# PSUM as a ring of four two-bank tiles, and a rearranged head, in a convolution kernel made of lookups

## The chip, the core and the metric

The kernel runs on one core of one Trainium2 chip. Such a core has five engines that run at the same time, each through its own list of instructions and strictly in the order of that list: TensorE (PE in the profile) multiplies matrices, VectorE (DVE) and ScalarE (ACT) work elementwise, GpSimd (POOL) too, and SyncE (SP) issues DMAs. PE has a second row, PEld, for loading the weights that stay in the array during a matmul. PE writes only to PSUM, a small memory of eight banks; here a bank holds 512 numbers of 32 bits on each of 128 partitions. The engines wait for one another by semaphores. The metric is the device time of one execution in microseconds (us).

## The reference

The input x has 16 images of 256 channels and 28x28 pixels. A group norm is followed by two "lookup" convolutions with batch norms, a squeeze-and-excitation gate and two residual sums:

```
def amm_conv3x3(x, centroids, w_sub):          # centroids: 256 channels, k=16, s=9
    p = 3x3 patches of x                       # per channel and pixel: 9 numbers
    d = |p|^2 - 2 p.centroids + |centroids|^2  # distance to each of 16 centroids
    attn = softmax(-d)                         # over the 16
    lut = einsum('cks,cso->cko', centroids, w_sub)
    return einsum('bnck,cko->bno', attn, lut)

out = amm_conv3x3(group_norm(x), centroids1, w_sub1)
out = relu(batch_norm1(out))
out = amm_conv3x3(out, centroids2, w_sub2)
out = batch_norm2(out)
out = out * sigmoid(relu(mean(out) @ w1 + b1) @ w2 + b2)
return x + relu(out + group_norm(x))
```

## The kernel before

**The work is cut into blocks.** A block is one layer, one image, one half of the channels (`hh`) and one half of the image's rows (`t`, 14 rows, 392 pixels, the `N` of the code). There are 2 x 16 x 4 = 128 blocks. The list `blocks` numbers them from 0; I call them block 0, block 1 and so on. The four blocks of one image and layer are needed together, because the sum over the channels is done by a Strassen-like scheme with seven products in place of eight.

**What happens to a block.** `patches` reads the shifted rows of the normalised image, which lies in HBM in `home1` or `home2`, into one of two tiles `pts` in SBUF, six DMAs for each half block. `logits` makes the 16 distances of a quarter of the block's channels: 16 small matmuls, each in a 32x32 corner of the array, into four PSUM banks. `exps` takes the exponential on ACT, bank by bank, and so frees the banks. `num_b` sums the exponentials (the denominators of the softmax, and the ninth tap); `split_b` on ACT and `join_b` on DVE sort the two apart, `recip_dve` inverts, `spread` shuffles the reciprocals to the right partitions. `num_a` makes the other eight taps' numerators, a quarter of the channels at a time, into two banks. They leave PSUM by `copy_a` on ACT (scaled later by `scale_q` on POOL) or by `scale_a` on DVE, scaled on the way. The results are the tiles `q`. `mix` subtracts q tiles of two blocks on POOL, `product` multiplies q tiles by weights (18 matmuls for a full one) into one accumulator bank, and `acc_copy` or `acc_add` takes it out.

**PSUM.** All of these take their banks from one pool, `p_ring`, by `bank(name)` (L103): eight tiles of one bank, handed out in turn. Whoever takes the next tile waits until the tile that was handed out eight turns earlier has been read.

**The order is written out by hand.** `at(cl, sub, f, ...)` (L847) files a job under a step `cl` and a place `sub` within it. At the end all jobs are issued in the order of (step, place), and this is the order in each engine's list. A block takes two steps: in each, `logits` and `exps` for two quarters (places 0.1 to 0.22). Block j starts at step 2j. Its `num_b` comes at step 2j+2, place 1.3, two `num_a` at 1.35, `split_b` 1.4, `copy_a` 1.45, `join_b` 1.5, `recip_dve` 1.6; its other two `num_a` come at step 2j+3, place 1.0, with `scale_a` at 1.1 and the `scale_q` of the first two at 1.8. A `product` stands at place 2.0 of most steps. So an even step has two `logits`, a `num_b`, two `num_a` and a product, an odd step two `logits`, two `num_a` and a product.

**The next image's group norm** is threaded into this: `load_x` (SP), `gn_stats` (DVE), `gn_mean` and `gn_var` (a small matmul each, DVE, and in `gn_var` also POOL: `rsqrt`, L235 and L236, then L317 and L318), `gn_apply` on ACT with what POOL made, and `to_home1` on SP, which writes the normalised image to HBM. The patches of the image's first block read it back.

**The head.** Before the first logits the program loads image 0 in two halves, normalises each (`norm0`), centres the centroids of the two channel halves (`center_wd`: squares on DVE, matmuls with `nhalf_sb` on PE, sums on DVE), fills the `pts` tiles with ones and writes image 0 to `home1`. In before, `center_wd(1)` stands at step 0, place 1.95, the weights `A11` of the first product are loaded at step 1, and image 1 at step 2.

## Time and profile before

| what | value |
|---|---|
| median of three runs | 2734.56 us (2731.55 to 2735.21) |
| the profiled execution | 2732.52 us, its span 2731.0 us |
| PE busy | 2663.6 us, 98% of the span |
| POOL busy | 2075.3 us, 76% |
| DVE busy | 1718.3 us, 63% |
| ACT busy | 1445.9 us, 53% |
| granted PE clock, mean | 0.995 |

The span runs from the first to the last instruction; 1.5 us of the profiled execution lie outside it. A row of the timeline view has the start, the time that the row's instructions covered, the engine, the line of the kernel, the operation, what it writes and reads, how many instructions were merged into the row, and in brackets how long the engine had been idle before them and what ended that. Matmul ends are modelled in the profile, so a busy PE is not necessarily a PE at its peak. `<-issue` means that the profile shows nothing that the engine waited for.

### The profile page before, as it was taken

The page shows a single profiled execution, that of the slowest core. Times are in us where ns is not written, and L with a number is a line of the kernel's source. Part 1 is how long each engine was busy: PE and PEld are TensorE (multiplying, and loading weights), DVE is VectorE, ACT ScalarE, POOL GpSimd, SP SyncE. Part 2 cuts the span into 40 slices and gives each one's busy share as a digit, 9 for nine tenths or more (in the row PEclk, how much of TensorE's full clock was granted, in tenths as well). Part 3 has the DMA queues.
Part 4 walks back from the last instruction along what each step waited for, and adds up shares of the span by engine and source line. Part 5 has one row for each costly group of instructions (what it writes and reads, how often), then busy time and mean ns, then how long its engine had stood idle before and what let it go on. Part 6 is the DMA issues. An engine that isn't in the chain of part 4 may idle for free. (4 is left out here: it accounts for less than half of the span.)

```text
span 2731.0 us, 87796 instructions
## 1 busy us (share of the span) xinstructions
PE 2663.6 (98%) x36984; PEld 1293.3 (47%) x36984; DVE 1718.3 (63%) x3943; ACT 1445.9 (53%) x3233; POOL 2075.3 (76%) x1425
## 2 busy tenths in 40 slices
PE   5899999999999999999999999999999999999998
PEld 2444544444444444444444444444444444444444
DVE  4765655566565556655567766666766676766674
ACT  3445444544445554555545555656556656556653
POOL 4856787766887677876678887788887788887787
PEclk9999999999999999999999999999999999999999
DMA  9665667766566666666585555545555445555441
GB/s 198 150 143 159 144 156 197 190 148 129 151 163 160 172 155 140 172 166 160 127 180 119 106 121 121 115 102 116 115 122 125 111 105 115 115 124 125 110 105 57
DMA packets 223624, 374.50 MB, mean 137 GB/s; under 512 B 30633, under 2 KB 194009, under 8 KB 223225
## 3 DMA queue, kind: packets, MB, share of 16 engines
q1 hardware_dynamic: 216280, 334.87, 53.3%
q0 software_dynamic: 6944, 33.95, 3.7%
q8 instruction: 295, 4.83, 0.8%
q14 instruction: 105, 0.85, 0.1%
HBM read 288.93 MB, written 79.80 MB: 135 GB/s over the span
## 5 line engine op out<-in xcount | busy, mean ns | idle before, releaser
L369 ACT ACTIVATE e<-lg 128x392 f32<-128x392 f32 x1920 | 778.2, 528 | 803.9 <-PE lg L357 797.7
L495 POOL TENSOR_TENSOR qp<-qp,qp 128x784 f32<-128x784 f32 x512 | 938.2, 1861 | 26.0 <-DVE qp L478 26.0
L486 PE MATMUL acc<-qp,w_S 128*128 128x392 f32 x2048 | 704.4, 494 | 0.9 <-POOL qp L495 0.9
L467 POOL TENSOR_TENSOR qp<-qp,rb 128x784 f32<-128x784 f32 x256 | 471.5, 1859 | 181.3 <-DVE rb L459 173.5
L357 PE MATMUL lg<-pt,wd 32*32 32x392 f32 x16384 | 541.2, 504 | 21.1 <-DMA pt<-home 16.2
L459 DVE STREAM_SHUFFLE rb<-r 128x392 f32<-128x392 f32 x1024 | 551.7, 603 | 0.0
L486 PEld LDWEIGHTS acc<-qp,w_S 128*128 128x128 f32 x2048 | 386.7, 190 | 299.1 <-issue 17.4
L486 PE MATMUL acc<-qp,w_A 128*128 128x392 f32 x1536 | 521.2, 492 | 0.0
L438 DVE SCALAR_TENSOR_TENSOR r<-nb,kst,r 128x392 f32<-128x392 f32 x128 | 79.8, 624 | 572.9 <-ACT r L429 557.6
L404 PE MATMUL na<-e,cwa 64*32 64x392 f32 x8192 | 412.1, 495 | 9.0 <-issue 9.0
L486 PEld LDWEIGHTS acc<-qp,w_A 128*128 128x128 f32 x1536 | 291.8, 190 | 213.8
L418 PE MATMUL nb<-e,cwb 64*32 64x392 f32 x8192 | 373.8, 496 | 3.9 <-issue 3.4
L467 POOL TENSOR_TENSOR qo<-qo,rb 128x392 f32<-128x392 f32 x128 | 131.0, 1024 | 301.6 <-DVE rb L455 301.4
L357 PEld LDWEIGHTS lg<-pt,wd 32*32 32x32 f32 x16384 | 232.8, 103 | 257.3 <-issue 170.9
L444 DVE RECIPROCAL r<-r 128x392 f32<-128x392 f32 x128 | 331.9, 2593 | 0.0
L478 DVE TENSOR_TENSOR qp<-na,rb 128x392 f32<-128x392 f32 x512 | 253.3, 554 | 68.4 <-PE na L404 58.9
L404 PEld LDWEIGHTS na<-e,cwa 64*32 64x32 f32 x8192 | 147.0, 106 | 236.4 <-ACT e L369 122.0
L418 PEld LDWEIGHTS nb<-e,cwb 64*32 64x32 f32 x8192 | 144.1, 107 | 226.2 <-issue 140.5
L472 ACT COPY qp<-na 128x392 f32<-128x392 f32 x512 | 211.8, 513 | 9.1 <-PE na L404 9.1
L429 ACT ACTIVATE r<-nb,kst 128x392 f32<-128x392 f32 x128 | 87.6, 684 | 105.6 <-PE nb L418 100.8
L375 ACT COPY e<-lg 128x392 f32<-128x392 f32 x128 | 52.9, 501 | 149.8 <-PE lg L357 149.8
L493 POOL TENSOR_TENSOR qo<-qo,qo 128x392 f32<-128x392 f32 x128 | 130.8, 1022 | 1.7
(149 smaller groups left out, 1747.9 us busy)
## 6 DMA issues: line engine op xcount, KB each, us to landing
pt<-home SPq DMA_DIRECT2D x768, 209.0 KB
pt<-home SPq DMA_DIRECT2D x756, 104.5 KB
home<-xpad SPq DMA_DIRECT2D x31, 899.0 KB
xt<-in_x SPq DMA_DIRECT2D x30, 784.0 KB
out_dram<-y SPq DMA_DIRECT2D x32, 392.0 KB
w_S<-d_wS SPq DMA_DIRECT2D x4, 576.0 KB
st<-in_wsub SPq DMA_DIRECT2D x4, 512.0 KB
st<-d_wa SPq DMA_DIRECT2D x16, 128.0 KB
```

Source lines behind the costliest of these rows:

```text
L357: nc.tensor.matmul(bk[32 * c : 32 * c + 32, :N].rearrange("p (r w) -> p r w", w=W), lhsT=wts["wd", u["hh"]][32 * i : 32 * i + 32, mm, c, : ...
L369: nc.scalar.activation(eg[:, i, :], bk[:, :N], AF.Exp, scale=2.0)
L404: nc.tensor.matmul(bs[r][32 * i : 32 * i + 32, :N], lhsT=wts["cwa", u["hh"]][64 * r : 64 * r + 64, mm, i, :], rhs=es[64 * r : 64 * r + 64, ...
L418: nc.tensor.matmul(bs[r][32 * i : 32 * i + 32, :N], lhsT=wts["cwb", u["hh"]][64 * r : 64 * r + 64, mm, i, :], rhs=es[64 * r : 64 * r + 64, ...
L444: nc.vector.reciprocal(u["r"], u["r"])
L459: nc.vector.stream_shuffle(rb[:, r, :], u["r"], mask_of(2 * mm + r))
L467: nc.gpsimd.tensor_tensor(q, q, u.pop(("rb", mm)), ALU.mult)
L472: nc.scalar.copy(u["q", 2 * mm + r], bk[:, :N])
L478: nc.vector.tensor_mul(u["q", 2 * mm + r], bk[:, :N], rb[:, r, :])
L486: nc.tensor.matmul(accs[key][:, :N], lhsT=wl[w][:, k, :], rhs=us["q", k], start=first and n == 0, stop=last and n == len(ks) - 1,)
L493: nc.gpsimd.tensor_tensor(out_u["q", 8], in0["q", 8], in1["q", 8], ALU.subtract)
L495: nc.gpsimd.tensor_tensor(pair(out_u, mm), pair(in0, mm), pair(in1, mm), ALU.subtract)
```

## The change

The pool `p_ring` has four tiles of two banks in place of eight tiles of one. `logits`, `num_a` and `num_b` put two banks' worth into one tile, and `exps`, `wide_copy`, `copy_a` and `scale_a` read both banks (128x784) with one instruction where two read one bank each (128x392). Everything else that asks for a bank (`product`, the group norm's sums, the centring, the gate) now gets a two-bank tile and uses its first bank. The matmuls stay the same, in the same banks of a group.

In the head, the weights `A11` are loaded at the start and the second half of `cwa` and `cwb` at step 4, the other way round from before. The tile `pts[1]` is filled by ACT, not POOL. The centring of the second half is cut in two, the squares ahead of step 0 and the rest in step 1. Block 0's `num_b` and all that follows from it comes one step earlier (step 1 where it was step 2; its other `num_a` at step 2 where they were at 3). Image 1 is loaded at the end of step 3 (before: step 2), its `gn_stats` and `gn_mean` stand at step 5 (before: 4), its `gn_var` at step 6, place 0.25 (before: step 4, place 2.2), `gn_apply` at step 6, place 0.3 (before: step 5, place 0.3), and both `to_home1` at step 6, place 0.4 (before: step 5, places 0.9 and 1.9).

The diff, without its plainly repeated parts:

```diff
--- before.py
+++ after.py
@@ -94,14 +94,17 @@
     const = ctx.enter_context(tc.tile_pool(name="const", bufs=1))
     dram = ctx.enter_context(tc.tile_pool(name="dram", bufs=1, space=DRAM))
     small = ctx.enter_context(tc.tile_pool(name="small", bufs=2))
-    p_ring = ctx.enter_context(tc.tile_pool(name="p_ring", bufs=8, space=PSUM))
+    p_ring = ctx.enter_context(tc.tile_pool(name="p_ring", bufs=4, space=PSUM))
 
     gmat = const.tile([P, P], F32, name="gmat")
     make_block_diagonal(nc, gmat, 8)
     ctx.enter_context(tc.manual_schedule())
 
+    def banks(name):
+        return p_ring.tile([P, 2, 512], F32, tag="ps", name=name)
+
     def bank(name):
-        return p_ring.tile([P, 512], F32, tag="ps", name=name)
+        return banks(name)[:, 0, :]
 
     def view(t, off, dims):
         return bass.AP(t.tensor, t.offset + off, [list(d) for d in dims])
@@ -193,7 +196,7 @@
     kst = load(konst, "kst")
     load_cw(0, 0)
     load_wd(None, 1)
-    load_cw(0, 1)
+    load_w(0, "A11")
     vecs = load(vec, "vecs", nc.gpsimd)
     w1_sb = const.tile([P, NB, 2 * RED], F32, name="w1_sb")
     w2_sb = const.tile([2 * RED, P], F32, name="w2_sb")
@@ -352,7 +355,9 @@
     def logits(u, mm):
         bs = []
         for i in range(4):
-            bk = bank("lg")
+            if i % 2 == 0:
+                bs.append(banks("lg"))
+            bk = bs[-1][:, i % 2, :]
             for c in range(4):
                 nc.tensor.matmul(
                     bk[32 * c : 32 * c + 32, :N].rearrange("p (r w) -> p r w", w=W),
@@ -360,19 +365,18 @@
                     rhs=u["pt", mm // 2][32 * i : 32 * i + 32, 4 * (mm % 2) + c, :].rearrange("p (r w) -> p r w", w=PW)[:, :, :W],
                     start=True, stop=True,
                 )
-            bs.append(bk)
         u["lg", mm] = bs
 
     def exps(u, mm):
         eg = epool.tile([P, 4, N], F32, tag="e", name="e")
         for i, bk in enumerate(u.pop(("lg", mm))):
-            nc.scalar.activation(eg[:, i, :], bk[:, :N], AF.Exp, scale=2.0)
+            nc.scalar.activation(eg[:, 2 * i : 2 * i + 2, :], bk[:, :, :N], AF.Exp, scale=2.0)
         u["e", mm] = eg
 
...
@@ -397,12 +401,12 @@
         nc.scalar.activation(eg, eg, AF.Exp, scale=2.0)
 
     def num_a(u, mm):
-        bs = [bank("na") for _ in range(2)]
+        bs = banks("na")
         es = u["e", mm]
         for i in range(4):
             for r in range(2):
                 nc.tensor.matmul(
-                    bs[r][32 * i : 32 * i + 32, :N],
+                    bs[32 * i : 32 * i + 32, r, :N],
                     lhsT=wts["cwa", u["hh"]][64 * r : 64 * r + 64, mm, i, :],
                     rhs=es[64 * r : 64 * r + 64, i, :],
                     start=True, stop=True,
@@ -410,13 +414,13 @@
         u["na", mm] = bs
 
     def num_b(u):
-        bs = [bank("nb") for _ in range(2)]
+        bs = banks("nb")
         for mm in range(4):
             es = u["e", mm]
             for i in range(4):
                 for r in range(2):
                     nc.tensor.matmul(
-                        bs[r][32 * i : 32 * i + 32, :N],
+                        bs[32 * i : 32 * i + 32, r, :N],
                         lhsT=wts["cwb", u["hh"]][64 * r : 64 * r + 64, mm, i, :],
                         rhs=es[64 * r : 64 * r + 64, i, :],
                         start=(mm == 0), stop=(mm == 3),
@@ -424,7 +428,7 @@
         u["nb"] = bs
 
     def split_b(u):
-        b0, _ = u["nb"]
+        b0 = u["nb"][:, 0]
         r = rpool.tile([P, N], F32, tag="r", name="r")
         nc.scalar.activation(r, b0[:, :N], AF.Identity, bias=zero, scale=m_hi)
         q = qs["one"][u["qi", 4]]
@@ -433,7 +437,7 @@
         u["q", 8] = q
 
     def join_b(u):
-        _, b1 = u.pop("nb")
+        b1 = u.pop("nb")[:, 1]
         r, q, w = u["r"], u["q", 8], u["w"]
         nc.vector.scalar_tensor_tensor(
             r, b1[:, :N], m_lo, r, op0=ALU.mult, op1=ALU.add, accum_out=wsum[:, w : w + 1]
@@ -467,15 +471,15 @@
         nc.gpsimd.tensor_tensor(q, q, u.pop(("rb", mm)), ALU.mult)
 
     def copy_a(u, mm):
-        for r, bk in enumerate(u.pop(("na", mm))):
+        for r in range(2):
             u["q", 2 * mm + r] = pair(u, mm)[:, r, :]
-            nc.scalar.copy(u["q", 2 * mm + r], bk[:, :N])
+        nc.scalar.copy(pair(u, mm), u.pop(("na", mm))[:, :, :N])
 
     def scale_a(u, mm):
         rb = u.pop(("rb", mm))
-        for r, bk in enumerate(u.pop(("na", mm))):
+        for r in range(2):
             u["q", 2 * mm + r] = pair(u, mm)[:, r, :]
-            nc.vector.tensor_mul(u["q", 2 * mm + r], bk[:, :N], rb[:, r, :])
+        nc.vector.tensor_mul(pair(u, mm), u.pop(("na", mm))[:, :, :N], rb)
 
     accs = {}
 
@@ -884,21 +888,22 @@
                     at(g + 1, 0.9, wide_exp, u, mm)
                 else:
                     at(g + p, 0.12 + 0.1 * q, exps, u, mm)
-        at(g + 2, 1.3, num_b, u)
-        at(g + 2, 1.4, split_b, u)
-        at(g + 2, 1.5, join_b, u)
-        at(g + 2, 1.6, recip_dve, u)
-        at(g + 2, 1.7, spread, u, 4)
-        at(g + 2, 1.71, scale_q, u, 4)
+        h = g + 2 if j else 1
+        at(h, 1.3, num_b, u)
+        at(h, 1.4, split_b, u)
+        at(h, 1.5, join_b, u)
+        at(h, 1.6, recip_dve, u)
+        at(h, 1.7, spread, u, 4)
+        at(h, 1.71, scale_q, u, 4)
         for mm in range(2):
-            at(g + 2, 1.35, num_a, u, mm)
-            at(g + 2, 1.45, copy_a, u, mm)
-            at(g + 3, 1.8 + 0.01 * mm, spread, u, mm)
-            at(g + 3, 1.8 + 0.01 * mm, scale_q, u, mm)
+            at(h, 1.35, num_a, u, mm)
+            at(h, 1.45, copy_a, u, mm)
+            at(h + 1, 1.8 + 0.01 * mm, spread, u, mm)
+            at(h + 1, 1.8 + 0.01 * mm, scale_q, u, mm)
         for mm in range(2, 4):
-            at(*((g + 2, 1.8) if mm == 2 else (g + 3, 0.05)), spread, u, mm)
-            at(g + 3, 1.0, num_a, u, mm)
-            at(g + 3, 1.1, scale_a, u, mm)
+            at(*((h, 1.8) if mm == 2 else (h + 1, 0.05)), spread, u, mm)
+            at(h + 1, 1.0, num_a, u, mm)
+            at(h + 1, 1.1, scale_a, u, mm)
 
     for l in range(2):
         for b in range(B):
@@ -942,14 +947,14 @@
                         for r in range(2):
                             at(g + 12 + o + (o and r), (1.72, 2.9)[r] if o == 0 else (1.805, 2.9)[r], to_home2, b, o, r)
                 if b + 1 < B:
-                    at(*((g - 1, 2.6) if b else (2, 1.65)), load_x, b + 1)
+                    at(*((g - 1, 2.6) if b else (3, 1.66)), load_x, b + 1)
                     for q in range(NB):
-                        at(g + (1 + q if b else 4), 0.3, gn_stats, b + 1, q)
-                    at(g + (3 if b else 4), 2.1, gn_mean, b + 1)
-                    at(g + 4, 2.1 if b else 2.2, gn_var, b + 1)
+                        at(g + (1 + q if b else 5), 0.3, gn_stats, b + 1, q)
+                    at(g + (3 if b else 5), 2.1, gn_mean, b + 1)
+                    at(*((g + 4, 2.1) if b else (6, 0.25)), gn_var, b + 1)
                     for q in range(NB):
-                        at(g + 5, 0.9 if b else 0.3, gn_apply, b + 1, q)
-                        at(g + 5, 1.9 if b or q else 0.9, to_home1, b + 1, q)
+                        at(*((g + 5, 0.9) if b else (6, 0.3)), gn_apply, b + 1, q)
+                        at(*((g + 5, 1.9) if b else (6, 0.4)), to_home1, b + 1, q)
             else:
                 last = b == B - 1
                 at(*((g + 11, 0.6) if last else (g + 13, 2.6)), load_x, b, last)
@@ -970,7 +975,7 @@
                     at(g + 11, 0.65, flags)
                     at(g + 12, 2.9, flag_sum)
 
-    at(1, 1.65, load_w, 0, "A11")
+    at(4, 0.6, load_cw, 0, 1)
     at(3, 1.65, load_w, 0, "S3")
     at(3, 1.65, load_w, 0, "A22")
     at(6, 0.6, load_w, 0, "A12")
@@ -1030,20 +1035,34 @@
         gn_var(0, k, 1)
         gn_apply(0, k)
 
-    def center_wd(hh):
-        center(wts["wd", hh].rearrange("p a b c -> p (a b c)"), 512)
+    def flat_wd(hh):
+        return wts["wd", hh].rearrange("p a b c -> p (a b c)")
+
+    squares = []
+
+    def center_wd1(part):
+        wf = flat_wd(1)
+        if part == 0:
+            squares.extend(center_sq(wf, c0, 256) for c0 in (0, 256))
+        else:
+            for c0 in (0, 256):
+                center_add(wf, c0, 256, squares[c0 // 256])
+            center_mean(wf, 512)
 
     nc.vector.memset(pts[0][:, :4], 1.0)
+    nc.scalar.activation(
+        pts[1], xpads[0][:, :PTW].unsqueeze(1).to_broadcast([P, 8, PTW]), AF.Identity, bias=1.0, scale=1.0
+    )
     norm0(0)
     for i in range(2):
         to_home1(0, 0, i)
     nc.vector.memset(pts[0][:, 4:], 1.0)
-    nc.gpsimd.memset(pts[1], 1.0)
-    center_wd(0)
+    center(flat_wd(0), 512)
     norm0(1)
-    at(0, 1.95, center_wd, 1)
     at(-0.5, 0.7, to_home1, 0, 1)
-    at(0, 1.96, setup_bn)
+    at(-0.4, 0.7, center_wd1, 0)
+    at(1, 1.25, center_wd1, 1)
+    at(1, 1.96, setup_bn)
     for t in hpads:
         at(1, 1.95, nc.gpsimd.memset, t, 0.0)
 ```

## The prediction

> **What bounds the kernel now.** I read the page first: which engine is full, and where along the span.
>
> ```profile
> PE 2663.6 (98%) x36984; PEld 1293.3 (47%) x36984; DVE 1718.3 (63%) x3943; ACT 1445.9 (53%) x3233; POOL 2075.3 (76%) x1425
> ...
> PE   5899999999999999999999999999999999999998
> ```
>
> PE is busy in every slice but the first ones and the last; 67 us of its span are idle. Second, the waits of PE alone, cut at 205 us. Up to there:
>
> ```profile
> PE lg L357 <- DMA pt<-home: 14.5, 4, 8.0
> PE gnp L298 <- DVE gn_mv L293: 9.1, 2, 5.7
> PE na L404 <- issue: 7.8, 4, 4.1
> ...
> PE acc L486 <- POOL w_S L188: 3.7, 1, 3.7
> ```
>
> and after it:
>
> ```profile
> PE lg L357 <- DVE hpad L523: 3.5, 4, 1.3
> PE nb L418 <- issue: 3.4, 2, 1.8
> ```
>
> The second list has 13 us in all. So visible idle time is to be had in the first 200 us only, and what the ring does to the other 2500 us must lie inside the busy time. Third, therefore, the timeline of one ordinary odd step:
>
> ```profile
> 1130.57 2.03 PE L357 MATMUL lg<-pt,wd 32*32 32x392 f32 x64
> 1131.56 3.23 ACT L369 ACTIVATE e<-lg 128x392 f32<-128x392 f32 x8 [5.48 <-PE lg L357]
> 1132.53 0.18 PEld L404 LDWEIGHTS na<-e,cwa 64*32 64x32 f32 x16 [0.64 <-ACT e L369]
> ...
> 1134.10 0.93 PE L486 MATMUL acc<-qo,w_S 128*128 128x392 f32 x2
> ```
>
> The first `num_a` starts 1.96 us after the logits, behind an ACT exponential that frees its banks. But in 52 of 119 even steps after 205 us `num_b` also starts at 1.96, although ACT began 0.06 earlier there (0.93 against 0.99 after the logits). So the usual limit is the logits' own end, 2.03, less 0.07; the exponentials come next, close behind.
>
> Fourth, POOL and ACT around the place to which the next image's `gn_var` moves:
>
> ```profile
> 67.80 0.22 POOL L235 TENSOR_SCALAR rs_t<-gn_var 128x2 f32<-128x2 f32 x1 [2.47 <-DVE nrm L315]
> ...
> 73.65 4.82 POOL L467 TENSOR_TENSOR qp<-qp,rb 128x784 f32<-128x784 f32 x2 [4.22 <-ACT xpad L324]
> 78.41 1.03 POOL L493 TENSOR_TENSOR qo<-qo,qo 128x392 f32<-128x392 f32 x1
> 79.38 8.42 POOL L495 TENSOR_TENSOR qp<-qp,qp 128x784 f32<-128x784 f32 x4
> 87.75 1.03 POOL L467 TENSOR_TENSOR qo<-qo,rb 128x392 f32<-128x392 f32 x1
> ```
>
> POOL goes without a gap from 73.65 to 119.84. In before, `gn_var` passes ahead of that, while POOL is idle.
>
> **Part 1: evacuation by pairs.** Eight exponentials take 3.23 us, one 0.53, so they start (3.23 - 0.53)/7 = 0.39 apart; two banks one by one are done 0.39 + 0.53 = 0.92 after the first starts. The nearest row for a pair is ACT's 128x784 ReLU from SBUF, 0.91 each, two in 1.66: 0.75 apart. A pair must wait for both banks; in the first `logits` call they finish 0.027 us apart. So the first pair is free at 0.03 + 0.91 = 0.94 against 0.92, no change. The second is free at 0.03 + 0.75 + 0.91 = 1.69 by that row, against 3 x 0.39 + 0.53 = 1.70. The first exponential of a run takes 0.50, not 0.53, and the ReLU's mean is that of queued ones (0.84 when it isn't), so 0.07 less is possible. On the odd step the second `num_a` starts 0.05 after its fourth bank is free: gain 0 to 0.07 a step, or a loss of 0.03 if the pair's start is all that changes. I take 0.03: 118 odd steps after 205 us give 3.5 us.
>
> [...]
>
> The second `logits` call of a step is issued one instruction at a time: its first matmuls start 0.017 apart inside a group of four and 0.043 apart where a group's first weight load waits for a bank. In steps with a ninth wait the last group starts at 1.161, not 1.135. A wait thus costs 0.026, and two of this call's four go: up to 0.05 off the logits' end in all 237 later steps, or 0 if the group change itself is slow. I take 0.025, since in odd steps the exponential holds `num_a` anyway: 6 us, bounds 0 and 12.
>
> **Part 2: one-bank users take two.** The accumulator's tile comes round again after four tiles, at the second call's third group, where it came at the fourth. `acc_add` covers this: 0.57 us on DVE, done 0.68 after the logits start in the step shown, 0.3 before it is needed. Where `acc_copy` sits in ACT's queue behind other work (17 steps, last group at 1.54) or the group norm's or gate's small DVE work is ahead (last group at 1.19), one more group waits, 0.07 each; some 50 such steps: 3 us, bounds 0 and 6. Behind the waiting matmul are `num_a` or `num_b`, and behind them the product.
>
> `scale_a` and `copy_a` by pairs: DVE's four took 1.98, ACT's four 1.64, off PE's path; a product uses them one step later. Nothing; without that cover the second half of a pair still comes no later than now.
>
> Parts 1 and 2: -3.5 - 6 + 3 = -6 us, bounds -20 and +10.
>
> **Part 3: loads and block 0.** `A11` is 576 KB where 512 KB stood, at some 200 GB/s 0.3 us more, ahead of the home write issued at 12.13; bounds 0 and 1 on the first logits at 26.11. POOL's 2.89 us memset goes to ACT, which is idle from 2.3 to 11.06; a 128x1568 exponential takes 1.58, so twice as much 3.3: hidden.
>
> The second logits waited until 32.68 for the centring's two matmuls (1.2 each, with DVE between); their patches had landed at 30.9. After: 31.2 + 3.3 = 34.5; centring 2.4, 36.9 (the exponentials end 4.8 after the logits start, 36.0); `num_b` 3, `num_a` 1.5, block 1's logits 2.2, block 0's `num_a` 1.6, logits 2.1: 47.3, where before it is 50.04. Then block 2's logits need patches, in before at 52.77. They can be issued when block 1's first logits are done, 43.6, and no longer stand behind `A11`: 2 us to start and 5.4 to move (the time that they took after `A11`) is 51.0. Gain 1.8. PE's idle 3.7 us before it leave it at the slow clock, as 2.7 do in before (3.33 for the logits there, 2.03 later), so what follows costs the same. The two group-norm matmuls between 66.27 and 67.50 move away: 1.2 more. Step 5 starts at 64.5, step 6 at 51.0 + 19.6 = 70.6 (before 72.35), because the same DMAs lie between as before. Bounds of the gain at step 6: 0 and 4. Block 0's `split_b`, `copy_a`, reciprocal, shuffles and `scale_q` fall where ACT, DVE and POOL have gaps (POOL is idle from 39.8 to 41.4 and from 43.1 to 49.9), so they cost nothing; nor do `setup_bn`'s four short POOL and seven DVE instructions of 0.16 to 0.7 each at step 1, which nothing needs before step 11. Past SP's queue: `cw` at step 4 is needed at 6, image 1 needed at step 5 lands at about 65, just in time.
>
> **Part 4: `gn_var` behind the mixes.** At (6, 0.25) its four POOL instructions stand behind the `scale_q` of (5, 1.8) and five mixes of (5, 2.5). POOL starts the former 6.15 after step 5: 70.7; 4.8 + 1.0 + 8.4 make 84.9, the four instructions (67.80 to 69.43) 86.5; `gn_apply` 2.0 on ACT, 88.5. In ACT's queue behind it stand block 2's `split_b`, `copy_a`, `acc_copy` and step 7's exponentials; behind `split_b` wait `join_b`, and PE's next logits for that tile. 88.5 + 1.2 + 0.6 = 90.3 for step 7, before 82.81. `to_home1` goes out at 87.5 (before 73.65). For image 0 the logits came 26.11 - 12.13 = 14.0 after; here a second half of 450 KB more goes ahead, 2 us: step 8 at about 103, before 90.49.
>
> Some comes back. POOL's next link, block 2's ninth tap, waits for `recip_dve` (2.6) and a shuffle (0.6): 93.5, before 87.75. So POOL is 5.7 late, while PE is 12 late, and PE's wait of 3.7 for `w_S` at step 9 goes: step 10 at 118.87 + 5.7 = 124.6. I keep +5.5 for parts 3 and 4 together; bounds 0 (POOL's stretch absorbs it) and +12 (nothing comes back).
>
> **Sum.** -6 + 5.5 = -0.5. The profiled execution took 2732.52 (span 2731.0 and 1.5 around it), 2.0 less than the median of the runs shown. By the one the sum is 2732.0, by the other 2734.1; I take 2733 us.
>
> **Rivals.** (a) Faster: the waits cost what they seem to, the pairs end 0.07 earlier, and the head loses only 2: -12 - 8 + 3 + 2 = -15, 2719 us. For it: each wait's 0.026; also 5.9 us of idle `<-issue` before 180 us could vanish with other code positions. Against: POOL's queue order.
> (b) Slower: the home write and patches of image 1. If the delay of 12 at step 8 isn't absorbed, and the ring gives half of what I take, 2734.6 + 12 - 3 = 2744. It decides when step 10 starts later than 128. Against: POOL, not PE, sets steps 8 to 10 in before.
> (c) Slower by the ring: pairs start 0.03 late, no wait was ever costly, and waits for accumulators come: 3.5 + 6 + 5.5 = 2749.
> (d) The ring changes nothing because the logits' end binds: the head alone, 2740, inside the forecast's case.
>
> **How the numbers follow.** Chances: forecast 0.40 (own range 2725 to 2740), (a) 0.33, (b) 0.17, (c) 0.10. Two runs of this kernel tell apart about 0.2%, 5.5 us. Faster: 0.1 + 0.3 = 0.40; same 0.33; slower 0.27. The range 2714 to 2750 reaches over both sides' cases, (a) with 5 to spare.
>
> **What would show it.** ACT's pair group with a mean near 0.85 to 0.95; logits' 64 matmuls in 1.98, not 2.03; the product 3.45 to 3.50 after an odd step's logits. POOL's L235 of image 1 after five mixes, near 85; ACT idle before L324 for 10 us; step 7 near 90, step 8 near 102, step 10 near 124. Wrong: if L235 comes early or steps 7 and 8 keep their times, part 4 falls; if the logits stay at 2.03, the wait's price falls.

## The result, and the profile after

The changed kernel is slower: 2751.19 us median of 5 runs (2745.19 to 2757.44) against 2734.56, a ratio of 1.0061 with a 95% interval of 1.0041 to 1.0081. That is 16.6 us, or 11 to 22 by the interval. Run again beside other kernels it stood at 1.0065 (1.0049 to 1.0081). The forecast was 2733.

The profiled execution took 2753.86 (span 2752.4), 21.3 more than that of the kernel before. The page's busy times and PE's slices:

```profile
PE 2669.8 (97%) x36984; PEld 1266.0 (46%) x36984; DVE 1697.6 (62%) x3687; ACT 1372.0 (50%) x1954; POOL 2071.5 (75%) x1424
...
PE   5889999999999999999999999999999999999998
```

ACT and DVE have less to do, as the change says. But PE's busy time rose by 6.2 us although its matmuls are the same, and its idle time rose from 67.4 to 82.6. So two things are to be found: 15 us in which PE waits, and some 6 in which it works more slowly.

The start of each step's first logits matmul says where. Differences to the kernel before, in us, by the profiled executions:

| step | 4 | 5 | 6 | 7 | 8 | 10 | 14 | 16 | 18 | 25 | 255 |
|---|---|---|---|---|---|---|---|---|---|---|---|
| before starts at | 52.77 | 67.50 | 72.35 | 82.81 | 90.49 | 118.87 | 165.16 | 191.04 | 215.28 | 289.92 | 2673.89 |
| after | +1.2 | +0.6 | +4.3 | +10.9 | +16.1 | +11.6 | +16.2 | +16.2 | +19.6 | +18.6 | +20.8 |

Sixteen of the 21 are there at step 8, and 2.5 more come by step 25. The other 230 steps, in which the ring was to gain, add 2.2. PE's waits up to 205 us:

```profile
PE lg L362 <- DMA pt<-home: 13.9, 3, 7.7
PE gnp L301 <- DVE gn_mv L296: 10.0, 3, 5.8
PE na L408 <- issue: 7.6, 1, 7.6
PE lg L362 <- DVE qp L482: 6.4, 1, 6.4
PE lg L362 <- ACT qp L476: 4.1, 1, 4.1
```

The two waits for `qp` (`scale_a` on DVE, `copy_a` on ACT) did not exist before; four stalls of `na` without a releaser have become one of 7.6. After 205 us:

```profile
PE na L408 <- issue: 6.0, 4, 2.9
PE lg L362 <- DVE hpad L527: 4.3, 4, 2.0
PE lg L362 <- ACT hpad L521: 3.3, 2, 2.0
PE lg L362 <- DMA pt<-home: 2.3, 1, 2.3
```

And the place to which `gn_var` moved, on POOL, ACT, SP and PE in the timeline:

```profile
80.93 7.28 POOL L499 TENSOR_TENSOR qp<-qp,qp 128x784 f32<-128x784 f32 x4
...
88.18 0.22 POOL L238 TENSOR_SCALAR rs_t<-gn_var 128x2 f32<-128x2 f32 x1
...
89.83 1.98 ACT L327 ACTIVATE xpad<-xt,nrm 128x784 f32<-128x784 f32 x2 [8.39 <-POOL nrm L321]
90.90 1.49 SPq L339 DMA_DIRECT2D home<-xpad  x2
91.71 0.66 ACT L433 ACTIVATE r<-nb,kst 128x392 f32<-128x392 f32 x1
...
93.69 3.66 PE L362 MATMUL lg<-pt,wd 32*32 32x392 f32 x64 [4.08 <-ACT qp L476]
```

The four small POOL instructions start when the mixes are done, ACT stands for 8.39 us in front of `gn_apply`, `copy_a` behind it is late, and PE's step 7 waits for that. After the wait PE is slow: its 64 logits matmuls take 3.66 us and not 1.98. By windows (columns: window, us, busy times, PE's granted clock, DMA share, GB/s) of the changed kernel, with the same steps of the kernel before under it:

```profile
77.00:94.00 17.00, 12.80 (x176) 4.83 (x152) 4.25 (x9) 7.24 (x10) 12.55 (x11) 0.70 0.31 90
94.00:107.00 13.00, 10.56 (x124) 4.40 (x124) 11.03 (x24) 3.84 (x6) 8.45 (x7) 0.76 1.01 255
```

```profile
72.00:83.00 11.00, 8.82 (x182) 4.53 (x198) 9.60 (x20) 7.49 (x17) 9.35 (x6) 1.00 0.78 243
83.00:91.00 8.00, 8.00 (x134) 3.86 (x118) 8.00 (x19) 3.63 (x9) 7.98 (x8) 1.00 0.93 200
```

A granted clock of 0.70 and 0.76 in place of 1.00 goes with the extra busy time, since matmuls behind these waits ran at half speed (the granted clock was 0.50 from 76.5 to 86 us and from 93.5 to 97.5). Behind the wait of 3.79 us at step 6 the logits and `num_b` took 3.38 and 5.46 us where 1.98 and 2.86 are usual, 4.0 more; behind the 4.08 us at step 7 the logits and `num_a` took 2.7 more, and behind the 2.44 us at step 8 the logits 1.3.

### The profile page after: what moved, and what is told of

Read it like the earlier page. It is cut to its first block, busy times and chain, and to the rows that moved or that the text cites. A ratio compares the mean times of both kernels' runs of the same rounds, so it can differ in the third digit from the quotient of the medians.

```text
span 2752.4 us, 85938 instructions
## 1 busy us (share of the span) xinstructions
PE 2669.8 (97%) x36984; PEld 1266.0 (46%) x36984; DVE 1697.6 (62%) x3687; ACT 1372.0 (50%) x1954; POOL 2071.5 (75%) x1424
## 2 busy tenths in 40 slices
PE   5889999999999999999999999999999999999998
## 3 DMA queue, kind: packets, MB, share of 16 engines
q8 instruction: 295, 4.83, 0.8%
## 4 chain that ended last, share of the span: by engine, by line
PE 92%; DVE 3%; DMA 2%; POOL 1%; issue 1%; SPq 0%; ACT 0%; ACTq 0%; POOLq 0%; DVEq 0%
PE acc L490 47%; PE lg L362 18%; PE nb L422 13%; PE na L408 13%; DMA home<-hpad,col 1%; POOL qp L499 1%; DMA pt<-home 1%; DVE r L448 1%; DVE rb L463 0%; SPq L346 0%; DVE qp L482 0%; SPq L350 0%; DMA cwa<-in_cwa 0%; PE sqp L267 0%; DVE gn_dv L308 0%
## 5 line engine op out<-in xcount | busy, mean ns | idle before, releaser
L373 ACT ACTIVATE e<-lg 128x784 f32<-128x784 f32 x960 | 718.0, 831 | 852.4 <-PE lg L362 849.9
L499 POOL TENSOR_TENSOR qp<-qp,qp 128x784 f32<-128x784 f32 x512 | 936.9, 1859 | 29.2 <-DVE qp L482 29.2
L490 PE MATMUL acc<-qp,w_S 128*128 128x392 f32 x2048 | 706.5, 495 | 0.6 <-POOL qp L499 0.4
L362 PE MATMUL lg<-pt,wd 32*32 32x392 f32 x16384 | 542.3, 508 | 40.6 <-DMA pt<-home 16.2
L490 PEld LDWEIGHTS acc<-qp,w_S 128*128 128x128 f32 x2048 | 386.6, 190 | 302.3 <-issue 13.3
L490 PE MATMUL acc<-qp,w_A 128*128 128x392 f32 x1536 | 521.2, 492 | 0.0
L408 PE MATMUL na<-e,cwa 64*32 64x392 f32 x8192 | 409.1, 498 | 13.7 <-issue 13.6
L490 PEld LDWEIGHTS acc<-qp,w_A 128*128 128x128 f32 x1536 | 291.8, 190 | 213.8
L422 PE MATMUL nb<-e,cwb 64*32 64x392 f32 x8192 | 376.1, 500 | 0.7 <-DVE half_sum L527 0.7
L362 PEld LDWEIGHTS lg<-pt,wd 32*32 32x32 f32 x16384 | 219.5, 103 | 289.7 <-issue 179.4
L482 DVE TENSOR_TENSOR qp<-na,rb 128x784 f32<-128x784 f32 x256 | 236.6, 961 | 67.0 <-PE na L408 57.7
L408 PEld LDWEIGHTS na<-e,cwa 64*32 64x32 f32 x8192 | 131.5, 106 | 256.9 <-ACT e L373 144.8
L422 PEld LDWEIGHTS nb<-e,cwb 64*32 64x32 f32 x8192 | 145.0, 108 | 222.8 <-issue 140.7
L476 ACT COPY qp<-na 128x784 f32<-128x784 f32 x256 | 195.9, 822 | 15.4 <-PE na L408 15.4
L433 ACT ACTIVATE r<-nb,kst 128x392 f32<-128x392 f32 x128 | 86.9, 679 | 121.8 <-PE nb L422 121.8
L379 ACT COPY e<-lg 128x784 f32<-128x784 f32 x64 | 48.9, 815 | 157.1 <-PE lg L362 157.1
```

Of the source, the lines that this page charges most:

```text
L362: nc.tensor.matmul(bk[32 * c : 32 * c + 32, :N].rearrange("p (r w) -> p r w", w=W), lhsT=wts["wd", u["hh"]][32 * i : 32 * i + 32, mm, c, : ...
L373: nc.scalar.activation(eg[:, 2 * i : 2 * i + 2, :], bk[:, :, :N], AF.Exp, scale=2.0)
L408: nc.tensor.matmul(bs[32 * i : 32 * i + 32, r, :N], lhsT=wts["cwa", u["hh"]][64 * r : 64 * r + 64, mm, i, :], rhs=es[64 * r : 64 * r + 64, ...
L422: nc.tensor.matmul(bs[32 * i : 32 * i + 32, r, :N], lhsT=wts["cwb", u["hh"]][64 * r : 64 * r + 64, mm, i, :], rhs=es[64 * r : 64 * r + 64, ...
L476: nc.scalar.copy(pair(u, mm), u.pop(("na", mm))[:, :, :N])
L482: nc.vector.tensor_mul(pair(u, mm), u.pop(("na", mm))[:, :, :N], rb)
```

## The experiments

Ratios are to the kernel before, run beside each, with 95% intervals; 0.0010 is 2.7 us. Beside the groups of runs the kernel before itself measured from 2726 to 2735 us, so times in us compare only within a group, and between groups the ratios do. "Step 8" is its start.

| run | ratio | step 8 |
|---|---|---|
| changed | 1.0061 (1.0041 to 1.0081) | 106.5 |
| changed, again | 1.0065 (1.0049 to 1.0081) | 106.2 |
| ring alone | 1.0014 (0.9998 to 1.0030) | 92.5 |
| changed head, no ring | 1.0013 (1.0000 to 1.0026) | 108.5 |
| changed, image 1 put back | 1.0010 (0.9999 to 1.0021) | 94.5 |
| changed, mixes behind `gn_var` | 1.0038 (1.0022 to 1.0054) | 99.7 |
| changed head, no ring, image 1 put back | 0.9986 (0.9976 to 0.9996) | 94.1 |
| the same, `setup_bn` put back | 0.9986 (0.9974 to 0.9998) | 95.8 |
| changed, code moved by 88 instructions | 1.0051 (1.0034 to 1.0068) | 108.8 |
| changed, image 1 put back, code moved | 1.0007 (0.9993 to 1.0021) | 96.3 |
| no ring, image 1 put back, code moved | 0.9997 (0.9986 to 1.0008) | 98.6 |
| changed head, no ring, code moved | 1.0019 (1.0006 to 1.0032) | 109.0 |
| changed, 64 matmuls in front | 1.0164 (1.0149 to 1.0180) | 133.2 |
| changed, image 1 put back, three pairs and two single banks | 1.0564 (1.0549 to 1.0580) | 97.6 |

### The ring alone, and the head alone

The ring's functions in the kernel before, and nothing else:

```
-    p_ring = ctx.enter_context(tc.tile_pool(name="p_ring", bufs=8, space=PSUM))
+    p_ring = ctx.enter_context(tc.tile_pool(name="p_ring", bufs=4, space=PSUM))
+    def banks(name):
+        return p_ring.tile([P, 2, 512], F32, tag="ps", name=name)
...
```

> The kernel before with the four two-bank PSUM tiles and the pair evacuations alone; loads, block 0, setup_bn and gn_var stay where before has them. Theory H (the loss is made in the head: step 8 starts 16 us later after the change, and 22 at the last step): step 8 at 90 to 91 as in before, ordinary odd steps 9.59 instead of 9.65, the gain of 0.06 on each of some 118 odd steps (7 us) eaten in part by waits such as the accumulators' (1.3 us once, at 1206) and by PE's own issue stalls, which were 6 us more in the changed kernel after step 25: 2728 to 2737 us, within 0.3% of before. Theory R (the ring itself is slower, rival (c) of the prediction): most of the loss stays, 2745 to 2751.

Measured 2738.0, ratio 1.0014. Theory R falls: the ring by itself is not the 16 us. But neither did it gain.

The second kernel is the changed one with those lines turned round.

> The changed kernel with before's eight one-bank tiles and single evacuations; the rearranged head stays. Theory H: step 8 at about 106, as with the ring, ordinary odd steps back at 9.65: 2745 to 2757 us. Theory R: 2731 to 2737, the time of before.

Measured 2736.7, ratio 1.0013, the number of theory R, though step 8 does start at 108.5. So theory H in its simple form falls too: the changed head with its late step 8 costs 1.3 thousandths, the ring alone 1.4, and both together 6.1. Something in the pair is more than the sum.

### Image 1 put back, in the changed kernel

```
-                    at(*((g - 1, 2.6) if b else (3, 1.66)), load_x, b + 1)
+                    at(*((g - 1, 2.6) if b else (2, 1.65)), load_x, b + 1)
...
-                    at(*((g + 4, 2.1) if b else (6, 0.25)), gn_var, b + 1)
+                    at(g + 4, 2.1 if b else 2.2, gn_var, b + 1)
...
```

> The changed kernel with image 1's load, statistics, gn_mean, gn_var, gn_apply and home writes back at before's steps (2 to 5); everything else as changed. Theory H with gn_var behind the mixes as the main cause: gn_apply runs before step 6's exponentials, ACT does not stand idle for 8 us, step 7 at 88 to 90 instead of 93.7, step 8 at 95 to 99 instead of 106.5: 2739 to 2745 us, 7 to 11 faster than the changed kernel's 2751. If the late patches of step 6 (3.8 us of wait) and setup_bn's wait at step 3 are what counts, and the home write is hidden by them: 2748 to 2752.

Measured 2738.0, ratio 1.0010: 14 us of the loss go, more than expected. The home write is issued at 75.13 instead of 90.90, step 7 starts at 84.5 and step 8 at 94.5. Step 6 too comes 2.2 us earlier (74.49 against 76.66): image 1's 784 KB load no longer stands in SP's queue right ahead of its patches.

### Only POOL's order

```
-                at(g + 5, 2.5, mix, us[0], mm, us[1], us[0])
+                at(*((g + 5, 2.5) if n else (6, 0.35)), mix, us[0], mm, us[1], us[0])
```

> The changed kernel with one edit: on POOL the first image's five mixes of block 1 are issued behind the four instructions of gn_var and not ahead of them; no other engine's order changes. Theory H: gn_var's POOL instructions start near 81 instead of 88.2, gn_apply near 82.5 instead of 89.8, step 7 at 88 to 90 instead of 93.7, step 8 at 98 to 100 instead of 106.5, and of these 6 to 8 us all or nearly all remain at the end: 2743 to 2746 us. The rival that POOL's own stretch sets the later steps and absorbs the order (the prediction's forecast): step 8 earlier, but step 10 within 2 us of 130.5, and the time stays at 2750 to 2752.

The four instructions of `gn_var` pass the five mixes on POOL; every other engine's list stays as it was. In its timeline:

```profile
81.62 0.22 POOL L238 TENSOR_SCALAR rs_t<-gn_var 128x2 f32<-128x2 f32 x1 [1.01 <-DVE nrm L318]
...
83.27 2.00 ACT L327 ACTIVATE xpad<-xt,nrm 128x784 f32<-128x784 f32 x2 [1.61 <-POOL nrm L321]
84.19 7.32 POOL L499 TENSOR_TENSOR qp<-qp,qp 128x784 f32<-128x784 f32 x4
84.36 1.49 SPq L339 DMA_DIRECT2D home<-xpad  x2
```

ACT waits 1.61 instead of 8.39. Step 7 starts at 90.2, step 8 at 99.7 and step 10 at 127.9 instead of 130.5, and the time is 1.0038: some 7 us of 17, give or take 6, as theory H gave. The forecast's absorption, by which POOL's own stretch would have swallowed such a delay, does not hold: moving 1.4 us of POOL's work ahead of 8 bought some 7 us at the end, and by the traces 10 us are still there at step 25 (298.5 instead of 308.5).

### Image 1 put back without the ring: the fourth corner

> Before's one-bank PSUM, the changed head, but image 1's load, statistics, gn_mean, gn_var, gn_apply and home writes at before's steps. Fourth corner of a square: with the ring, putting image 1 back took the time from 2751 to 2738; without the ring the changed head alone measured 2736.7 although its step 8 started 18 us late. Theory A (the late home write costs 13 us with or without the ring, and what gave 10 of the 13 back without the ring is independent of it): step 8 at 93 to 96, 2722 to 2727 us, faster than before. Theory C (what gave it back is chance of where PE's code blocks arrive late: 1.2 us of such stalls in that run, against 10.6 in before and 13.6 in the changed kernel; a kernel that is not late has them again): 2731 to 2738.

Measured 2726.2, ratio 0.9986. The number lies in theory A's range, but the kernel before measured 2729.6 beside it, and 2735.1 in the runs from which the ranges were made: 0.9986 of that is 2731.3, the fast end of theory C's range. The number settles neither theory, and A's premise, one price with or without the ring, is not borne out by the corners below (7 us and 14). The stalls that theory C names came back in part, 5.2 us against 1.2 with the late home write. This kernel, with before's one-bank PSUM, the changed order of the first loads and block 0's early denominators, and image 1 at its old place, is faster than the kernel before by 1.4 thousandths (0.4 to 2.4), 4 us. The four corners give the ring's price as 2.4 thousandths (7 us) with image 1 put back and 5.0 (14 us) with the late home write, and the late home write's price as 2.7 (7 us) without the ring and 5.3 (14 us) with it.

### The changed kernel again

> The changed kernel itself, for a second trace of it and more times beside the others. Theory C: steps 0 to 12 start within 0.5 us of the first trace; PE's idle time without a releaser stands again at the same counts of PE instructions (4034, 16322, 18627, 32707, 50882 in the first, all 256 times a whole number plus 194 or 195), but some of these stalls change by 1 to 5 us; median 2747 to 2754. Rival: the stalls come at other counts.

Median 2749.6, ratio 1.0065. Steps 0 to 8 start within 0.8 us of the first trace, steps 9 and 10 within 1.1. The stalls without a releaser stand at the same counts of PE's instructions (columns: count, us of idle time in the first and in the second trace):

```
 4034   7.56   7.13
16322   1.02    -
18627   1.29   2.76
32707   0.83   2.54
50882   2.91   2.85
others    -    1.9 (6850, 18115, 34499, 64963)
```

Counts take all of PE's instructions together, as the trace lists them: matmuls, weight loads and 1073 that its sequencer runs, such as waits for semaphores. All are 256 n + 194 or 195. The trace also lists what the DMA queue of instructions moved: on PE's queue 295 packets of 16384 bytes, about one per 256 of PE's instructions; PE went on 1.2 to 1.9 us after the end of such a packet, in every one of these stalls. So "issue" here means that the next block of code had not arrived.

### Moving the code

The first attempt put 64 one-column matmuls with all of `gmat` ahead of the first group norm.

```
+    warm = bank("warm")
+    for _ in range(64):
+        nc.tensor.matmul(warm[:, :1], lhsT=gmat, rhs=gmat[:, :1], start=True, stop=True)
```

> The changed kernel with 64 matmuls of one column ahead of the first group norm, in time in which PE waits anyway (it has nothing to do before 11 us); they shift PE's later instructions by 128 places, half a block of 256. Theory C: the stalls without a releaser stay at counts of 256 n + 194 to 196 and so move by 64 matmuls in the program; their sum changes, and the time with it, to anywhere between 2738 and 2755. Rival (the stall belongs to a place in the program, the num_a of step 14 and of step 174): it stays at that num_a, at counts 128 higher, and the time stays at 2749 to 2753.

It missed what it was for, in two ways. Each such matmul is two matmuls and two weight loads in the list, so 64 made 256 instructions, a whole block, and moved no block's begin in the program. And they took 27 us, where PE has work from 5.75 us on:

```profile
4.39 27.47 PE L1054 MATMUL warm<-gmat 128*128 128x1 f32 x128 [4.39 <-POOL gmat L230]
```

so the kernel measured 2776.0 (1.0164). The stalls of 6.0 and 0.7 us came at counts 4290 and 51138, which is 256 later and the same place in the program.

The second attempt used 22 matmuls on a 32x32 corner, 88 instructions, while PE waits for the first patches; the first step starts at 25.88, so they cost nothing.

```
+    fill = bank("fill")
+    for _ in range(22):
+        nc.tensor.matmul(fill[:32, :1], lhsT=gmat[:32, :32], rhs=gmat[:32, :1], start=True, stop=True)
```

> The changed kernel with 22 matmuls of one column on a 32x32 corner of gmat behind the first image's group norm, in the 7.7 us in which PE waits for the first patches. They make PE's stream 88 instructions longer at that point, so every block of 256 instructions begins 88 instructions earlier in the program (the 64 matmuls of the earlier run were 256 instructions, a whole block, and moved nothing but the start). Theory C (a 16 KB block of PE's code is asked for when PE enters the block before it, and stands behind whatever large transfers were issued before): in the changed kernel PE passes count 3778 at 181.44, just behind the home write issued at 180.77, and the block moves only at 192.58; with 88 instructions fewer to go PE passes it near 178, ahead of both home writes, so the 7.1 to 7.6 us stall at count 4034 goes. PE passes 50626 near 1860 and no longer behind the 784 KB load issued at 1862.5, so the 2.9 us stall at 50882 goes. Others may come: 2737 to 2746 us, 4 to 13 below the changed kernel. Rival (these stalls belong to the places in the program): both stay at their num_a, 2748 to 2753.

Both named stalls went, as theory C says, so they belong to the blocks and not to `num_a`. Stalls of code sum to 6.0 us where the two traces of the changed kernel had 13.6 and 17.2. What the late block goes with is visible in the order of two events. PE passes count 3778, the begin of the block before; SP issues image 2's home writes, twice 899 KB (us; the last column is the idle time at count 4034 or 4035):

```
kernel                     second home write   PE passes 3778   next block moves   idle
before                                164.54           165.28             176.10   4.12
ring alone                            167.89           169.93             180.62   7.54
changed                               180.77           181.44             192.58   7.56
changed, again                        180.91           181.29             192.20   7.13
changed, image 1 back                 166.52           169.04             177.74   5.44
changed, mixes behind gn_var          175.05           174.89             183.06   5.10
head alone                            180.72           180.39             181.41      0
changed, code moved                   179.79           175.47             178.43      0
```

In the two rows where PE passes the mark 0.33 us or more ahead of the second home write, the block moves within 1 to 3 us. In the others, where it passes after it or 0.16 us ahead, the block comes 8 to 11 us later. No run moved the home write alone.

Not every stall is of this kind: 2.98 us in the trace of the head alone, at count 3990, and 1.48 in that of before, at 3992, follow no packet and stay unexplained.

The time fell by little, 1.0051 against 1.0061 and 1.0065, 3 to 4 us where 4 to 13 were expected, which is not clear of noise; by its number, 2748.5, the rival holds. Of 7.9 us won in step 14 against the changed kernel's trace, 5.8 were lost in step 16 (4.1 came back in step 17). On DVE and PE:

```profile
202.70 0.71 DVE L617 SCALAR_TENSOR_TENSOR row<-row,score 128x256 f32<-128x256 f32 x1 [2.20 <-DMA row<-in_before]
203.45 1.94 DVE L620 SCALAR_TENSOR_TENSOR row<-row,score 128x256 f32<-128x256 f32 x1
...
205.96 0.57 DVE L527 TENSOR_TENSOR half_sum<-acc,half_sum 128x392 f32<-128x392 f32 x1
```

```profile
206.58 5.48 PE L422 MATMUL nb<-e,cwb 64*32 64x392 f32 x64 [3.75 <-DVE half_sum L527]
```

DVE now waits for the row of scores, `acc_add` stands behind it, PE waits 3.75 us for that accumulator and then runs `num_b` at half speed (5.48 instead of 2.86). The stall had hidden a transfer that was late anyway.

> The changed kernel with image 1 back at before's steps, and the same 22 small matmuls. Its stalls of code were 5.4 at count 4034, 2.9 at 16322, 1.2 at 32707, 2.5 at 50882. Theory C: those at 4034 and 50882 go (PE passes 3778 at 165.5, with the second home write issued at 166.5), new ones of 0 to 4 may come: 2728 to 2735 us, against 2738 without the fill. Rival: 2736 to 2740.

Measured 2737.3, ratio 1.0007 against 1.0010 without the fill. The stalls at 4034 and 50882 went here as well, and all stalls of code fell from 15.7 to 3.5, yet the time stayed: by its number the rival holds. After 285 us, waits for `acc_copy` rose from 3.1 to 7.1 us; the longest, in this kernel's timeline:

```profile
1029.30 0.49 ACT L521 COPY hpad<-acc 128x392 f32<-128x392 f32 x1 [7.67 <-DMA home<-hpad,col]
...
1029.84 1.56 PE L362 MATMUL lg<-pt,wd 32*32 32x392 f32 x16 [3.28 <-ACT hpad L521]
```

`acc_copy` may not overwrite `hpad` until an indirect home write has read it, and the logits' last group needs the accumulator's banks. With PE on time, this transfer is what is late next.

> One-bank PSUM, image 1 back, and the 22 small matmuls. Its only code stall of note was 3.75 at count 4035 (PE passed 3778 at 167.78, behind the home writes of 166.3 and 167.0). Theory C: that one goes, others of 0 to 6 may come, since this kernel had few of them: 2720 to 2730 us, against 2726 without the fill. Rival: 2726 as it was, with the stall at the same num_a.

Measured 2734.3, ratio 0.9997 against 0.9986 without the fill, a difference of 1.1 thousandths with an uncertainty of 1.5. The time lies outside the range, but the range came from runs beside which the kernel before took 2729.6 and not 2734.8; by the ratio it would be 2728.7 there, inside theory C's range, and the run does not decide. Its stalls of code went from 5.2 to 9.2, since a block now came late at count 4290 (3.66), where the second home write was issued at 173.99 and PE passed the mark ahead at 179.23. Moving the code took away one such stall and brought another.

### `setup_bn` put back

```
-    at(1, 1.96, setup_bn)
+    at(0, 1.96, setup_bn)
```

> As the run with one-bank PSUM and image 1 put back, and setup_bn at step 0 again. In the changed kernel DVE's first instruction of setup_bn stood 1.81 us at 44.79 and the rest followed POOL until 49.31, so scale_a and with it step 3's second logits call came at 51.21, after 6.4 us of PE's idle time. Theory B (this wait costs): step 4 starts at 51 to 52 instead of 54 and the time is 2 to 3 us below the run without this edit. Rival (the patches of step 4 land no earlier): step 4 within 0.5 us of 54, no difference.

Ratio 0.9986, the same as without the edit, and step 4 started at 56.97, later and not earlier. The wait for `scale_a` did shrink, from 3.86 us without the edit to 0.76, but step 4's last patches, issued at 48.52, landed at 56.66, where without the edit they were issued at 49.26 and landed at 54.35. So theory B's first step fails here: what the logits no longer waited for, step 4 waited for its patches. A price of 2 to 3 us would not show in these ratios (each uncertain by 1.0 to 1.2 thousandths), and in the changed kernel, where image 1's load does not stand ahead of these patches, the edit was not tried.

### Two banks for the accumulators only

The one-bank users got two banks of their own, and the pairs three tiles.

```
-    p_ring = ctx.enter_context(tc.tile_pool(name="p_ring", bufs=4, space=PSUM))
+    p_ring = ctx.enter_context(tc.tile_pool(name="p_ring", bufs=3, space=PSUM))
+    p_one = ctx.enter_context(tc.tile_pool(name="p_one", bufs=2, space=PSUM))
...
-        return banks(name)[:, 0, :]
+        return p_one.tile([P, 512], F32, tag="one", name=name)
```

> The changed kernel with image 1 back at before's steps, and its PSUM split: three two-bank tiles for lg, na and nb, and two one-bank tiles of their own for the accumulators and the other small users. It prices the second bank that the one-bank users take. With four shared pairs, after 285 us PE waited 3.1 us for acc_copy (ACT hpad) and 2.2 for acc_add (DVE hpad), and 3.0 for the latter in the head; in the kernel before 0.7, 2.2 and 1.3. Theory P (the accumulators' second bank costs what these waits show): the logits' waits for hpad go, odd steps stay at 9.59 or less, 2732 to 2736 us against 2738. Rival (with three pairs the logits wait for na's or nb's evacuation instead): new waits of the logits for qp or qo, odd steps above 9.65, 2740 or more.

Measured 2881.8, ratio 1.0564. The waits for `hpad` did go, but the rival holds, in a form neither theory named:

```profile
1180.25 2.82 PE L363 MATMUL lg<-pt,wd 32*32 32x392 f32 x64
...
1182.18 0.18 PEld L363 LDWEIGHTS lg<-pt,wd 32*32 32x32 f32 x16 [0.83 <-ACT e L374]
1183.00 1.55 PE L409 MATMUL na<-e,cwa 64*32 64x392 f32 x32
```

The logits take 2.75 to 2.82 us in nearly every step, not 1.97. A step's two `logits` calls fill four pairs; with three, the fourth stands until the first exponential has emptied its pair. The row of weight loads shows this wait, 0.83 us for ACT's `e`. PE's own row counts it as busy, since the ends of its matmuls are modelled and reach over the break: PE's list of waits after 285 us shows 2.7 us in all, and the kernel lost 150. It prices the ring's depth, not the accumulators' bank, which stays without a price of its own.

### Do the two halves amplify each other, wherever the code lies?

> One-bank PSUM with the whole changed head, and the 22 small matmuls. With the blocks moved, the two-bank ring with the late home write measured 1.0051 of before, with image 1 back 1.0007, one-bank with image 1 back 0.9997. Theory A (the ring and the late home write simply add): 0.9997 plus 0.0044, so 1.0041, 2745 us beside a before of 2734. Theory C (they amplify each other, whatever the place of the code blocks; unmoved the one-bank corner stood at 1.0013): 1.001 to 1.002, 2737 to 2740 us.

Measured 2735.4, ratio 1.0019. With the code moved, the square's corners are 0.9997, 1.0019, 1.0007 and 1.0051; the excess over the sum is 2.2 thousandths, and unmoved it was 2.6 (the changed kernel taken as the mean of 1.0061 and 1.0065). Half-widths of the intervals added in squares make these uncertain by 2.8 and 2.4, their mean of 2.4 by 1.8. So the ring and the late home write amplify each other by 7 us, give or take 5, if both squares are taken together; with the code moved alone the excess is not clear of noise, so that the place of the code blocks has no part in it is not shown. Why is not settled. All traces with the late home write start step 8 at 106 to 109; it is later that the two without the ring lose less, and after step 25 the ring's traces lose against the others with the home write late or early. One difference can be read before step 8: `copy_a` by pairs frees both of a pair's banks at once, so step 7's logits wait 4.1 and 6.9 us for `copy_a` behind `gn_apply` in the changed kernel's two traces; without the ring they wait 2.6 and 3.2 for the `split_b` before it. But step 8 comes no later for it.

## Why the prediction was wrong

Two steps failed. "Some comes back" in part 4 let the steps after 8 win back more than PE's idle time there, and parts 1 and 2 counted the ring as a gain of 6 us where the pairs of runs that differ in it alone show a loss of 3 to 14 (the smallest ones not clear of noise).

**What bounds the kernel.** Right for the head, where 16 of the profile's 21 us are lost by step 8. For the ring it was not: what it costs after that shows in part as waits, in the list that had 13 us before.

**Part 1, pairs and waits (-3.5 and -6).** The mechanism was right where it was measured, an ordinary odd step:

```profile
1149.83 1.98 PE L362 MATMUL lg<-pt,wd 32*32 32x392 f32 x64
...
1150.88 2.97 ACT L373 ACTIVATE e<-lg 128x784 f32<-128x784 f32 x4 [5.65 <-PE lg L362]
1151.76 1.61 PE L408 MATMUL na<-e,cwa 64*32 64x392 f32 x32
1152.47 0.19 PEld L408 LDWEIGHTS na<-e,cwa 64*32 64x32 f32 x16 [0.53 <-ACT e L373]
...
1153.30 0.93 PE L490 MATMUL acc<-qo,w_S 128*128 128x392 f32 x2
```

The logits take 1.98 and not 2.03, the second `num_a` runs on from 2.65 and not 2.71 (its first matmul stands at 2.64 in both), the product starts at 3.47 and not 3.53. ACT's pairs start (2.97 - 0.84)/3 = 0.71 apart, with 0.84 as the last pair's time, where the ReLU from SBUF had given 0.75. What failed is the count. (Its sum, too: -3.5 - 6 + 3 is -6.5, not -6.) I compared each step's shortest time over the 7 traces with four two-bank tiles (the split kernel and the 64 matmuls left out) and over the 6 with eight single banks. After step 25, 94 odd steps gained 0.05 and 14 of the second layer lost 0.19, all ending in a small matmul of the gate (why was not tried); of 115 even steps 36 gained 0.05 and 27 some 0.02, but 31 lost 0.03 and four lost 0.42 to 0.77, so that in sum they gained nothing. Together that is -1.5 us, not -9.5: a wait's 0.025 was taken for all 237 steps, and only part of the even ones show it.

**Part 2, the second bank (+3, 0 to 6).** The mechanism is there: after 285 us the logits wait 4.0 us for `acc_copy` in the mean of those 7 traces and 0.8 in the 6 without a ring. In the changed kernel's first 285 us waits for `acc_add` add 2.6 more. Some 6 us, the upper bound.

**Left out of parts 1 and 2: the code.** Rival (a) read 5.9 us of idle time `<-issue` before 180 us (7.8 by the list shown) as something that other code positions could take away, a gain. The same traces show PE's stalls `<-issue` after 285 us at 6.3 in the mean with the ring and 3.2 without, and the list of PE's instructions changed its length (75166 before, 75041 after), so that later blocks begin at other places of the program. That the ring must have more such stalls is not shown; a stroke of ill luck would look the same. Between step 25 and the end, traces with the ring fall 2.2 to 5.1 us further behind the trace of before, those without it gain 2.4 to 12.9 on it, some 10 us apart in the mean; some of that may come from the groups, between which the kernel before itself differed by up to 9 us. The three terms make -1.5 + 3.2 + 3.1 = 4.8 of it. Some 2 more stand at step 55, where layer 2's centroids are centred in such a tile: 11.3 us in five of the 7 traces, 9.7 in the other two, and 9.1 in all 6. The rest is not placed.

**Part 3, loads and block 0.** Step 5 was to start at 64.5 and step 6 at 70.6; they started at 68.1 and 76.7. Step 4 was to start at 51.0 and started at 53.97: of its patches the three that POOL issues went out from 48.67 on, behind POOL's memset and its part of `setup_bn`, and not at 43.6 as foreseen; the last landed at 53.66, 4.99 after the first was issued, where I had estimated 2 + 5.4. Step 3's second half, too, ended only at 53.65. Two more covers failed. DVE's part of `setup_bn`, called harmless, stood 4.5 us in DVE's queue ahead of `scale_a`, because its first instruction took 1.81 us beside POOL's memset (0.16 in before, with no memset beside it) and the others followed POOL; step 3's second half waited 6.44 us. And "the same DMAs lie between as before" was wrong: the 784 KB of image 1 had moved to just ahead of step 6's patches, 3.8 us of wait where before had 1.27. What the first is worth at the end stays open: its run, in another kernel, shows no gain, but only moved the wait. The load was only moved back together with `gn_var`, which gained 14 us where POOL's order alone gained 7; so up to 7 may be its and the earlier statistics'.

**Part 4, `gn_var` behind the mixes.** Every event came, in its order: POOL's `gn_var` at 88.2 (foreseen 84.9), ACT idle for 8.4 us (10), step 7 at 93.7 (90.3), step 8 at 106.5 (103), all some 3 late by part 3. The step that failed is "Some comes back". It let POOL set step 10, at 124.6, so steps 8 and 9 were to take 21.6 us. In before they took 28.4, of which PE stood idle for 5.6:

```profile
98.49 0.88 PE L404 MATMUL na<-e,cwa 64*32 64x392 f32 x12 [1.91 <-issue]
...
112.74 0.93 PE L486 MATMUL acc<-qo,w_S 128*128 128x392 f32 x2 [3.73 <-POOL w_S L188]
```

No more than these 5.6 could come back, and 4.5 did: after the wait at its start, step 8 and step 9 ran without another, and step 10 started at 130.45. PE set it, not POOL, whose next link, too, came at 97.46 and not 93.5. Then step 10 lost 4 us again, to a wait for `acc_add` and a `num_b` at the slow clock (0.50 granted from 134 to 140 us):

```profile
134.19 1.56 PE L362 MATMUL lg<-pt,wd 32*32 32x392 f32 x16 [1.93 <-DVE hpad L527]
135.68 5.26 PE L422 MATMUL nb<-e,cwb 64*32 64x392 f32 x64
```

Rival (b) named the point, a start of step 10 later than 128, and its price of 12; its sum of 2744 fell short because it gave the ring half of a gain that was a loss. Rival (c)'s sum, 2749, came nearest, in part by luck: it held the ring for a loss, but by pairs that are free later and waits that cost nothing, and the odd steps show the reverse.

**The sum.** -6 + 5.5 should have been, by the first square's corners, a ring of +7, a late home write of +7, a changed head without it of -4, and 7 for the two together: +17.

## What to carry to other kernels

A small instruction put behind a long one on an engine with its own queue is priced by who waits for its result, and by a chain through other engines: four POOL instructions of 1.4 us in all cost some 7 us behind five mixes. A gain measured in one clean step must be counted in every kind of step, and set against what the edit does to waits elsewhere, before it is multiplied. And where PE waits for nothing that the trace shows, look whether the place repeats at the same count of instructions: and whether a packet of the instruction queue ends just before it (1.2 to 1.9 us in the changed kernel's two traces): then it is code that is late, and the transfers issued just before are the first thing to look at. That moving them alone would help was not tried.

## What the runs showed of the hardware

- PE's instructions came in blocks of 256 over the DMA engines: in the changed kernel 75041 instructions, and on PE's queue of instructions 295 packets of 16384 bytes, 16384/256 = 64 bytes an instruction; the stalls of its two traces stood at counts of 256 n + 194 or 195. Where PE entered the block before behind the second of two transfers of 899 KB, or 0.16 us ahead of it, the next block came 8 to 11 us later, and PE stood 4.1 to 7.6 us; where it did so 0.33 us ahead of the second one, the block came 1.0 us later.
- In the traces of before and of the changed kernel the granted clock stood at 0.50 behind each of the waits of PE of 4.12 us (before, at 178.56), 3.79, 4.08, 6.44 and 7.56 us (changed, at 76.66, 93.69, 51.21 and 194.92); behind the 8.04 and 7.68 us ahead of their first logits it stood at 1.00. Shorter waits were followed by half speed in some places and not in others. After 1.93 us at step 10 `num_b` took 5.26 us where 2.86 is usual, and after 2.44 us at step 8 the logits took 3.30, both at a granted clock of 0.50; after the 3.73 us in before, at 112.74, the granted clock stayed at 1.00, and after 2.91 us in the changed kernel, at 1872.36, too. Which short waits cost the clock was not tried.
- A float32 matmul on all of the array with one column took 27.47/64 = 0.43 us, as two matmuls with two weight loads; it is no cheap filler.
